# Windows of the large convolutions loaded during the last image's own layers, and paired products for dt and the normaliser

## The chip, the cores and the metric

The kernel runs on 1 core of a Trainium2 chip. The metric is the device time of one execution in microseconds. Three runs of the kernel before took 5239.56 us in the median (5237.0 to 5242.91). All data are f32. The engines are PE (matrix products), PEld (its weight loads), DVE (vector), ACT (scalar), POOL (GpSimd) and SP, which only issues transfers. DMAs are issued by SP, by ACT and by POOL.

## The reference

`x` is (8, 384, 32, 32): eight images, 384 channels, 1024 pixels. Four layers follow each other.

```python
# layer 0: RMS norm, a selective scan over the 1024 pixels in both directions, a 3x3 depthwise gate
def mamba(x, ...):
    u, z = split(x @ in_proj.T);  u = silu(causal_conv1d(u, 4 taps) + b)
    dt, Bm, Cm = split(u @ x_proj.T, [24, 40])            # 24, 16, 16
    delta = softplus(dt @ dt_proj.T + dt_b)
    h = exp(delta * A) * h + (delta * u) * Bm              # 16 states, pixel after pixel
    return ((h * Cm).sum(states) + u * D) * silu(z) @ out_proj.T
x_norm = rmsnorm(x)
g = (mamba(x_norm) + flip(mamba(flip(x_norm)))) * scale_mod
x = x + res_scale * (g + sigmoid(dwconv3x3(x_norm)) * x_norm)
# layer 1: bn, 1x1, 3x3 depthwise, bn, 1x1, residual; linear attention of 8 heads; layer norm and MLP
x1 = conv1x1(bn(dwconv3x3(conv1x1(bn(x))))) + x
q, k, v = split(conv1x1(x1));  qp, kp = phi(q), phi(k)     # phi(t) = exp(.5 * (2t - t*t))
z = 1 / (qp . kp.sum(pixels) + eps)                        # the normaliser
x2 = x1 + conv1x1((qp @ (kp.T @ v)) * z)
x = x2 + gelu(ln(x2) @ w1 + b1) @ w2 + b2                  # 384 -> 1536 -> 384
# layer 2: seven depthwise convolutions (13x13, 5x5, 7x7, dilated ones), each with its bn, summed
x = sum(bn_j(dwconv_j(x)))
# layer 3: 1x1 with bn and residual, then 13x13 depthwise and a scale per channel, each with bn
xp = bn(conv1x1(x)) + x
out = gelu(bn(dwconv13x13(xp)) + bn(xp * dw1_w))
```

## The kernel before

Everything is in two functions. `tile_layers` makes the constants, calls `_layers01` for layers 0 and 1, and then computes layers 2 and 3 for all eight images at once.

**Layers 0 and 1, image by image.** `front(b)` makes what the scan of image b needs: the norm, `in_proj`, the local 3x3 gate, the short convolution, `x_proj` and, per half image and 128 channels, two products `dt` (one per direction, with 24 rows of weights each that lie at partitions 0 and 64), softplus, and delta (`dlt`) and delta times u (`vr`), which go to DRAM. `scan(b)` walks over units of a direction, a half image and 128 channels; each has four rounds of four states. A round loads `dlt`, `vr` and `bct` (B and C) in a form repeated over the states, and computes `da` (ACT, L782), `du` (DVE, L787), the scan `hs` (DVE, L799), `hs` times C (POOL, L808) and the sum over states `acc` (PE). `layer1(b)` then does the rest of layer 0 and layer 1: `op` (out_proj, added to `xx` by DVE at L891), `h` into the padded image `hh` (its edge columns are set by POOL in `image6`, L526; it is put into DRAM `h_d` by ACT, L532), the 3x3 depthwise `dw` from `dw_i` (SP loads, L543), `c2`, keys and values, queries, the normaliser `den` (six products at L1005, for the two half images in two column groups of PE), its reciprocal `rz` and the product `rzb` (L1017) that spreads it over the channels, `pj`, the layer norm, and the MLP (`mf`, `hm`, `mo`), whose result goes to DRAM `x2_d` (POOL, L1070).

**What sets the order.** Each engine's order is made by the scheduler of the Tile framework from the order in which the program is written and from the buffers of the pools. A planner in `_layers01` writes it: it steps through the scans of images 0 to 7, and between rounds it advances generators (`front(b+1)`, `layer1(b-1)`, `fold`, `prepare`) whose costs and due times are in `jobs`. `defer` and `tick` put small DVE work some steps later. `together(products, made)` keeps a list of products side by side on PE: the first is held behind the instructions `made`, and the others follow with a high priority (`AHEAD`) in program order. Before the change it is used for the 32-column products (`col32`), for `x_proj` and for `acc`. Image 7's `layer1` has no other image beside it:

```python
        tick(everything=True)
        for _ in seconds[B - 1]:
            tick()
        tick(everything=True)
```

**Layers 2 and 3.** During image 1's scan `kernels` (driven as `prepare`) merges layer 2's seven kernels into one 13x13 kernel per channel, in DRAM as `g2_d`, and layer 3's 13x13 and its scale as `g3_d`. A convolution `conv(g_d, src_d, tag, put)` runs over 96 groups of 4 channels. `xt` holds rows of the images (32 rows on 32 partitions, loaded by POOL at L281, then copied by DVE at L289 to three more blocks of 32 partitions, each shifted by a column). `tp` holds the Toeplitz windows, which the load makes out of the kernel by overlapping reads from DRAM in runs of 512 bytes, two blocks by SP and two by ACT. Both tiles cover 16 channels and have three buffers. A group is 16 products (4 taps, 4 channels, 32 columns each; they count twice in the profile) into one of six PSUM tiles `cv`. Convolution a reads `x2_d` and stores `yt` to `y2_d` (POOL, L319). The pointwise stage follows in 16 steps: a load `yp` (SP), nine products `pw` (L333), `tm` (ACT), the residual into `xo` (DVE; the three `xo` tiles are set to zero by POOL at L243 ahead of convolution a), and a store to `xp_d` (POOL, L347). Convolution b reads `xp_d`, and each group ends with a gelu into `ot` (ACT, L353, three buffers) and a store to `out` in runs of 128 bytes (POOL, L354). `pbias`, a small bias product, stands ahead of convolution a.

The tiles of these stages come out of pools that are opened after those of `_layers01` are closed, so they lie in the same memory and have to wait for its last users.

Of the kernel before, what the change touches and what calls it, by code (L numbers as in the profile page):

```python
# [10 lines left out]
FP = mybir.dt.float32  # L11
# [28 lines left out]
N_A6, N_T2, N_S2, N_W, N_IM = 7, 9, 3, 4, 8  # L40
N_REP, N_DA, N_HS = 6, 4, 8
# [26 lines left out]
def tile_layers(  # L68
# [95 lines left out]
    def kernels(small, large):  # L164
# [60 lines left out]
        with nc.allow_non_contiguous_dma(reason="384 biases"):  # L225
# [3 lines left out]

    _layers01(tc, nc, B, xv, x2_d, dram, ident, mean_w, eps5, eps6, one, half, minus1, vec, bns, bnt,  # L230
              rs, rsm, inproj_t, xproj_t, dtproj_t, outproj_t, taps1, taps3, taps3b, sel, alog,
              cw1_t, cw2_t, qkv_t, proj_t, w1, w2, headmask, mask8, mask8_t, kernels)
# [4 lines left out]
    with tc.tile_pool(name="cw", bufs=1) as cwp, tc.tile_pool(name="cx", bufs=2) as cxp, tc.tile_pool(  # L237
        name="cps", bufs=6, space=PSUM
# [11 lines left out]

        pbias = cwp.tile([P, NC, 1], FP, tag="pbias", name="pbias")
        for m in range(NC):
            ps = cps.tile([P, HALF], FP, tag="cv", name=f"pb_{m}")
            for k in range(NC):
                nc.tensor.matmul(
                    ps[:, 0:1], pwt[:, k, m * P : (m + 1) * P], bias2[:, k, :],
                    start=(k == 0), stop=(k == NC - 1),
                )
            nc.vector.scalar_tensor_tensor(
                pbias[:, m, :], ps[:, 0:1], bns("pw", m), bnt("pw", m), ALU.mult, ALU.add  # L260
            )
            nc.vector.tensor_add(pbias[:, m, :], pbias[:, m, :], bias2[:, m, :])

        def conv(g_d, src_d, tag, put):
# [3 lines left out]
            NCH = 4 * GB  # L268
            xt = tp = None
            for g in range(NQ):  # L270
                if g % GB == 0:
                    xt = cxp.tile([P, NCH, RL], FP, tag="xt", name=f"xt_{tag}_{g}", bufs=3)
                    tp = cxp.tile([P, NCH, TP], FP, tag="tp", name=f"tp_{tag}_{g}", bufs=3)

                    q0 = g // GB % 2 * 2
                    at = [H * ((q0 + e) % NSH) for e in range(NSH)]
                    src = bass.AP(
                        src_d.tensor, src_d[4 * g, 0, 0].offset,
                        [[RL, H], [H * RL, NCH], [1, RL]],
                    )  # L280
                    nc.gpsimd.dma_start(xt[at[0] : at[0] + H], src)  # L281
                    for e in range(NSH):
                        win = bass.AP(
                            g_d.tensor, g_d[4 * g, e, 0, 0].offset,
                            [[KT, H], [NSH * TG * KT, NCH], [1, TP]],
                        )
                        (nc.scalar if e % 2 else nc.sync).dma_start(tp[at[e] : at[e] + H], win)
                    for n in (1, 2):
                        nc.vector.tensor_copy(  # L289
                            xt[at[n] : at[n] + n * H, :, 0 : RL - n - (n - 1)],  # L290
                            xt[at[0] : at[0] + n * H, :, n : RL - (n - 1)],
                        )
                ps = cps.tile([P, HALF], FP, tag="cv", name=f"cv_{tag}_{g}")
                for t in range(KT):
                    for e in range(4):
                        c = 4 * (g % GB) + e
# [25 lines left out]

        yf = y2_d.rearrange("(k p) h b w -> p k (h b w)", p=P)
        xf = xp_d.rearrange("(k p) h r -> p k h r", p=P)
        NB = 2 * BW
        for t in range(H // 2):
# [20 lines left out]
            nc.gpsimd.dma_start(xf[:, :, 2 * t : 2 * t + 2, :], xo)  # L347

# [12 lines left out]
def _layers01(tc, nc, B, xv, x2_d, dram, ident, mean_w, eps5, eps6, one, half, minus1, vec, bns, bnt,  # L361
              rs, rsm, inproj_t, xproj_t, dtproj_t, outproj_t, taps1, taps3, taps3b, sel, alog,
              cw1_t, cw2_t, qkv_t, proj_t, w1, w2, headmask, mask8, mask8_t, kernels):
# [10 lines left out]
    with ExitStack() as ctx:  # L374
        wp = ctx.enter_context(tc.tile_pool(name="w0", bufs=1))
        sp = ctx.enter_context(tc.tile_pool(name="s0", bufs=2))
        accp = ctx.enter_context(tc.tile_pool(name="acc0", bufs=1, space=PSUM))
# [196 lines left out]
        def front(b):  # L574
# [56 lines left out]
            for h in range(2):  # L631
# [37 lines left out]
                for c in range(NC):  # L669
                    dls = []  # L670
                    for d in range(2):
                        ps = psum(f"dt_{b}_{h}_{d}_{c}")
                        at = slice(64 * d, 64 * d + DTR)
                        nc.tensor.matmul(
                            ps, wdt[at, c * P : (c + 1) * P], xd[at, :], start=True, stop=True
                        )
                        dl = t2(f"dl_{b}_{h}_{d}_{c}")
                        nc.scalar.activation(dl, ps, AF.Softplus, bias=vec("dt_b", c))
                        dls.append(dl)
# [15 lines left out]
        def scan(b):  # L695
# [10 lines left out]
            def load_bc(k, r):  # L706
                d, h, _ = units[k]
                t = sp.tile([P, 2, HALF], FP, tag="bct", name=f"bct_{b}_{d}_{h}_{r}", bufs=4)
# [8 lines left out]
            def load(k, i):  # L717
# [3 lines left out]
                for src_d, n in ((dl_d, "dlt"), (v_d, "vr")):  # L721
                    t = sp.tile([P, 2 * HALF], FP, tag="rep", name=f"{n}_{b}_{d}_{h}_{c}_{i}", bufs=N_REP)
# [38 lines left out]
            for k, (d, h, c) in enumerate(units):  # L761
                cols = bass.ts(h, HALF)
                second = k % (2 * NC) >= NC
                for r in range(NR):
# [12 lines left out]
                    for i in range(2):  # L777
                        dlt, vt = now[i]
                        da = sp.tile([P, 2 * HALF], FP, tag="da", name=f"da_{b}_{k}_{r}_{i}", bufs=N_DA)
# [15 lines left out]
                        t = sp.tile([P, 2 * HALF], FP, tag="hs", name=f"hs_{b}_{k}_{r}_{i}", bufs=N_HS)  # L795
# [80 lines left out]
        def layer1(b):  # L876
# [126 lines left out]
            for k in range(NC):  # L1003
                for h, at in enumerate(ats):
                    nc.tensor.matmul(  # L1005
                        den[at, :], ksv[:, k, :], qps[h][:, k, :], start=(k == 0), stop=(k == NC - 1),
                        skip_group_check=True,
                    )
            for at in ats:
                nc.scalar.activation(rz[at, :], den[at, :], AF.Ln, bias=eps6[at])  # L1010
            for at in ats:
                nc.scalar.activation(rz[at, :], rz[at, :], AF.Exp, scale=-1.0)
            yield 3
            for k in range(NC):
                for h, at in enumerate(ats):
# [192 lines left out]
```

## Time and profile before

| | |
|---|---|
| runs shown | 5239.56 us median of 3 |
| the profiled execution | 5247.45 us, span 5245.7 us |
| instructions | 57987 |
| busy PE, PEld | 4292.2 us (82%), 1772.1 us (34%) |
| busy DVE, ACT, POOL | 3793.6 us (72%), 2739.8 us (52%), 2911.7 us (56%) |
| mean granted clock of PE | 0.9 |
| DMA | 975.07 MB, mean 186 GB/s |

The stages after the last scan, in us from the span's start, by the instructions of the tiles named:

| stage | from | to |
|---|---|---|
| image 7's own layers | 4207 | 4574 |
| convolution a, products `cv_a` | 4594.75 | 4814.15 |
| pointwise, products `pw` | 4827.84 | 4953 |
| convolution b, products `cv_b` | 4971.5 | 5241 |

How to read it: the page lists the busy time of each engine over the whole span, and that of 40 equal slices; a group of instructions is a source line, an engine, an operation and its tiles, with a count and the mean of one. A busy share over the whole span mixes stages that have different limits, so each stage is read by itself. A wait is given to the one that released it last. A DMA share over 1 means that the packets of a stretch took longer, summed, than 16 engines have time: packets in flight lie over one another.

### The profile page before, as it was taken

What the parts mean: (1) busy time and instruction counts of PE and PEld (TensorE: products, weight loads), DVE (VectorE), ACT (ScalarE), POOL (GpSimd) and SP (SyncE); (2) the same over time, 40 slices, a digit from 0 to 9 for tenths busy, and PEclk for the clock granted to TensorE, in tenths of its full rate; (3) what the DMA queues carried; (4) which work ended last, traced back from release to release, by engine and by line L of the source; (5) the groups of instructions that cost most, each with busy time, mean ns of one, the idle gap of its engine ahead of it and who ended that gap; (6) DMA issues with size and microseconds to landing.
All of it is one profiled execution on the core that took longest, in us unless ns stands there. A gap on an engine that the chain in (4) does not pass through costs nothing. (4 is left out here: it accounts for less than half of the span.)

```text
span 5245.7 us, 57987 instructions
## 1 busy us (share of the span) xinstructions
PE 4292.2 (82%) x20128; PEld 1772.1 (34%) x20128; DVE 3793.6 (72%) x3765; ACT 2739.8 (52%) x3816; POOL 2911.7 (56%) x1472
## 2 busy tenths in 40 slices
PE   4675568888988998898889888998788879787877
PEld 1121123233333333333333333333233324365455
DVE  0399899987888788878887889788879901065344
ACT  1455544785578557755775677468536603001211
POOL 3276666676667665766675667566767800111155
PEclk7686679899989998999899999999889999899988
DMA  9866447666757674767567646765644541499698
GB/s 280 253 198 209 167 146 217 205 202 177 213 190 208 177 222 168 224 179 218 176 199 203 213 168 196 211 204 183 160 150 137 147 105 38 79 235 219 193 197 168
DMA packets 560045, 975.07 MB, mean 186 GB/s; under 512 B 53208, under 2 KB 238024, under 8 KB 559752
## 3 DMA queue, kind: packets, MB, share of 16 engines
q1 hardware_dynamic: 410992, 669.13, 42.8%
q0 software_dynamic: 56800, 205.10, 15.2%
q10 hardware_dynamic: 91960, 97.14, 6.8%
q8 instruction: 159, 2.61, 0.2%
q14 instruction: 134, 1.10, 0.1%
HBM read 726.36 MB, written 244.81 MB: 185 GB/s over the span
## 5 line engine op out<-in xcount | busy, mean ns | idle before, releaser
L808 POOL TENSOR_TENSOR hs<-hs,bct 128x1024 f32<-128x1024 f32 x768 | 2410.7, 3139 | 1001.1 <-DVE carry L804 470.6
L782 ACT ACTIVATE da<-dlt,neg_a 128x512 f32<-128x512 f32 x1536 | 1035.6, 715 | 775.7 <-DVE hs L799 718.5
L799 DVE TENSOR_TENSOR_SCAN hs<-da,du 128x512 f32<-128x512 f32 x768 | 902.4, 1209 | 248.7 <-ACT da L782 146.3
L787 DVE TENSOR_TENSOR du<-vr,bct 128x1024 f32<-128x1024 f32 x768 | 1059.3, 1379 | 29.0 <-DMA vr<-v_d 18.5
L799 DVE TENSOR_TENSOR_SCAN hs<-da,carry,du 128x512 f32<-128x512 f32 x768 | 944.1, 1267 | 56.4 <-PE acc L506 14.4
L506 PE MATMUL acc<-hs,selt 128*32 128x512 f32 x2304 | 560.5, 658 | 189.8 <-POOL hs L808 189.7
L1058 PE MATMUL mo<-hm,w 128*128 128x512 f32 x1152 | 572.0, 637 | 91.1 <-ACT hm L1056 89.4
L489 PE MATMUL mf<-ln,w 128*128 128x512 f32 x1152 | 565.6, 627 | 11.7 <-DMA w<-w_d 11.7
L501 PE MATMUL acc<-hs,selt 128*32 128x512 f32 x768 | 419.5, 645 | 72.8 <-POOL hs L808 46.8
L1058 PEld LDWEIGHTS mo<-hm,w 128*128 128x128 f32 x1152 | 219.4, 200 | 438.3 <-issue 240.3
L782 ACT ACT_TABLE_LOAD x278 | 356.7, 1283 | 7.6 <-ACT hh L899 2.7
L489 PEld LDWEIGHTS mf<-ln,w 128*128 128x128 f32 x1152 | 222.4, 200 | 334.3 <-issue 314.3
L489 PE MATMUL in<-xn,win 128*128 128x512 f32 x576 | 293.0, 640 | 12.0 <-ACT uz L603 7.7
L301 PE MATMUL cv_b<-xt_b,tp_b 128*32 128x256 f32 x3072 | 203.9, 424 | 83.3 <-ACT ot L353 60.6
L1070 POOL DMA_DIRECT2D x_d<-xx x48 | 56.4, 1177 | 350.6 <-DVE xx L1067 350.5
L289 DVE COPY xt_b<-xt_b 32x4992 f32<-32x4992 f32 (+1 forms) x48 | 135.0, 2813 | 131.8 <-DMA xt_b<-xp_d 131.0
L1056 ACT ACTIVATE hm<-mf,biasf 128x512 f32<-128x512 f32 x192 | 131.9, 687 | 179.6 <-PE mf L489 177.8
L301 PE MATMUL cv_a<-xt_a,tp_a 128*32 128x256 f32 x3072 | 182.3, 389 | 47.0 <-issue 37.1
L506 PE MATMUL dw<-dw_i,t3b 96*32 96x512 f32 x1056 | 207.5, 637 | 4.1 <-DMA dw_i<-h_d 3.6
L301 PEld LDWEIGHTS cv_b<-xt_b,tp_b 128*32 128x32 f32 x3072 | 150.8, 143 | 136.8 <-ACT ot L353 71.2
L506 PEld LDWEIGHTS acc<-hs,selt 128*32 128x32 f32 x2304 | 92.7, 114 | 301.3 <-POOL hs L808 281.0
L354 POOL DMA_DIRECT2D out<-ot x96 | 130.4, 1363 | 113.4 <-ACT ot L353 113.1
(194 smaller groups left out, 5771.4 us busy)
## 6 DMA issues: line engine op xcount, KB each, us to landing
dlt<-dl_d SPq DMA_DIRECT2D x384, 256.0 KB, 4.2
vr<-v_d SPq DMA_DIRECT2D x384, 256.0 KB, 4.9
bct<-bc_d SPq DMA_DIRECT2D x256, 256.0 KB, 3.8
ut<-u_d SPq DMA_DIRECT2D x192, 257.5 KB, 5.6
lc_i<-xn_d SPq DMA_DIRECT2D x192, 228.8 KB, 5.5
dw_i<-h_d SPq DMA_DIRECT2D x192, 228.8 KB, 4.5
w<-w_d SPq DMA_DIRECT2D x64, 576.0 KB, 6.1
w<-in_w SPq DMA_DIRECT2D x64, 576.0 KB, 5.4
```

The costliest lines, as they stand in the source:

```text
L289: nc.vector.tensor_copy(xt[at[n] : at[n] + n * H, :, 0 : RL - n - (n - 1)], xt[at[0] : at[0] + n * H, :, n : RL - (n - 1)],)
L301: nc.tensor.matmul(ps[H * e : H * (e + 1), 0:BW], tp[:, c, :].rearrange("p (j t) -> p j t", t=KT)[:, :, t], rhs, start=(t == 0), stop=(t = ...
L354: nc.gpsimd.dma_start(ov[g * P : (g + 1) * P], ot.rearrange("p (b w) -> p b w", w=W))
L489: nc.tensor.matmul(ps, w[:, k, m * P : (m + 1) * P], rhs[k] if isinstance(rhs, list) else rhs[:, k, :], start=(k == 0), stop=(k == NC - 1),)
L501: first = product()
L506: tc.keep_in_program_order(product())
L782: nc.scalar.activation(da[:, bass.ts(j, HALF)], dlt[:, bass.ts(j, HALF)], AF.Exp, scale=neg_a[:, g, r : r + 1],)
L787: nc.vector.tensor_mul(pairs(du), pairs(vt), bct[r][:, 0:1, :].to_broadcast([P, 2, HALF]),)
L799: nc.vector.tensor_tensor_scan(t[:, s][:, way], da[:, s][:, way], du[:, s][:, way], k_c if second else 0.0, ALU.mult, ALU.add,)
L808: made.append(nc.gpsimd.tensor_mul(pairs(t), pairs(t), bct[r][:, 1:2, :].to_broadcast([P, 2, HALF])))
L1056: nc.scalar.activation(hm, ps, AF.Gelu, bias=biasf[:, NC * i + f, :])
L1058: nc.tensor.matmul(acc[m], wb[:, f, m * P : (m + 1) * P], hm, start=(i == 0 and f == 0), stop=(i == FF // C - 1 and f == NC - 1),)
```

## The change

It does four things.

1. The scan's tiles `bct`, `rep`, `da` and `hs` move from the pool `s0` to a pool `scan` of their own, on the right side of the memory. That pool is closed before image 7's `layer1`. A pool `win` is opened in its place, with 20 tiles of 8 channels (`N_WIN`, `NCH`).
2. A generator `windows` loads the first 20 windows of convolution a through POOL's queue, advanced once per step of image 7's `layer1`.
3. `conv` takes windows of 8 channels, and `xt` of 8 channels with four buffers (before: 16 channels and three buffers for each). It asks for windows up to ten blocks ahead through SP and ACT. The pointwise loop asks for one window of convolution b per step. `pbias` is moved behind convolution a. The pools `cw`, `cx` and `cps` are opened with `reuse_waits="tile"`: each of their tiles waits for the users of its own place and not for those of the whole pool.
4. The two `dt` products, the six of `den` and the two `rzb` of each k go through `together`.

The core of the diff (the body of `put2`, of the products' loop and of `conv`'s addresses is moved unchanged, and left out):

```diff
+N_WIN, NCH = 20, 8
+    NB_C = C // NCH
+    wins = {}
+    def load_windows(g_d, tag, n, queues):
+        if not wins:
+            wins["pool"] = ctx.enter_context(tc.tile_pool(name="win", bufs=1, side="right"))
+        tp = wins["pool"].tile([P, NCH, TP], FP, tag="tp", name=f"tp_{tag}_{n}", bufs=N_WIN)
+        for e in range(NSH):
+            at = H * ((n % 2 * 2 + e) % NSH)
+            win = bass.AP(
+                g_d.tensor, g_d[NCH * n, e, 0, 0].offset,
+                [[KT, H], [NSH * TG * KT, NCH], [1, TP]],
+            )
+            queues[e % len(queues)].dma_start(tp[at : at + H], win)
+        wins[tag, n] = tp
+
+    def windows(queues):
+        for n in range(N_WIN):
+            load_windows(g2_d, "a", n, queues)
+            yield
...
-    with tc.tile_pool(name="cw", bufs=1) as cwp, tc.tile_pool(name="cx", bufs=2) as cxp, tc.tile_pool(
-        name="cps", bufs=6, space=PSUM
+    with tc.tile_pool(name="cw", bufs=1, reuse_waits="tile") as cwp, tc.tile_pool(
+        name="cx", bufs=2, reuse_waits="tile"
+    ) as cxp, tc.tile_pool(
+        name="cps", bufs=6, space=PSUM, reuse_waits="tile"
     ) as cps:
...
         def conv(g_d, src_d, tag, put):
-            NCH = 4 * GB
             xt = tp = None
             for g in range(NQ):
-                if g % GB == 0:
-                    xt = cxp.tile([P, NCH, RL], FP, tag="xt", name=f"xt_{tag}_{g}", bufs=3)
-                    tp = cxp.tile([P, NCH, TP], FP, tag="tp", name=f"tp_{tag}_{g}", bufs=3)
+                n, first = divmod(4 * g, NCH)
+                if first == 0:
+                    xt = cxp.tile([P, NCH, RL], FP, tag="xt", name=f"xt_{tag}_{n}", bufs=4)
                     ...
                     nc.gpsimd.dma_start(xt[at[0] : at[0] + H], src)
-                    for e in range(NSH):
-                        win = bass.AP(...)
-                        (nc.scalar if e % 2 else nc.sync).dma_start(tp[at[e] : at[e] + H], win)
+                    for m in range(n, min(n + 1 + N_WIN // 2, NB_C)):
+                        if (tag, m) not in wins:
+                            load_windows(g_d, tag, m, [nc.sync, nc.scalar])
+                    tp = wins[tag, n]
...
             nc.gpsimd.dma_start(xf[:, :, 2 * t : 2 * t + 2, :], xo)
+            if t < N_WIN:
+                load_windows(g3_d, "b", t, [nc.scalar, nc.sync])
...
+        scan_ctx = ExitStack()
+        scanp = scan_ctx.enter_context(tc.tile_pool(name="scan", bufs=1, side="right"))
...
-                    for d in range(2):
-                        ps = psum(f"dt_{b}_{h}_{d}_{c}")
-                        at = slice(64 * d, 64 * d + DTR)
-                        nc.tensor.matmul(
-                            ps, wdt[at, c * P : (c + 1) * P], xd[at, :], start=True, stop=True
-                        )
+                    pss = [psum(f"dt_{b}_{h}_{d}_{c}") for d in range(2)]
+                    together([
+                        partial(
+                            nc.tensor.matmul, pss[d], wdt[64 * d : 64 * d + DTR, c * P : (c + 1) * P],
+                            xd[64 * d : 64 * d + DTR, :], start=True, stop=True,
+                        )
+                        for d in range(2)
+                    ], [])
+                    for d, ps in enumerate(pss):
                         dl = t2(f"dl_{b}_{h}_{d}_{c}")
...
-            for k in range(NC):
-                for h, at in enumerate(ats):
-                    nc.tensor.matmul(den[at, :], ...)
+            together([
+                partial(nc.tensor.matmul, den[at, :], ksv[:, k, :], qps[h][:, k, :], ...)
+                for k in range(NC) for h, at in enumerate(ats)
+            ], [])
...
-                nc.scalar.activation(rz[at, :], rz[at, :], AF.Exp, scale=-1.0)
+                made = nc.scalar.activation(rz[at, :], rz[at, :], AF.Exp, scale=-1.0)
             yield 3
             for k in range(NC):
-                for h, at in enumerate(ats):
-                    ps = long_psum(f"rzb_{b}_{h}_{k}")
-                    nc.tensor.matmul(ps, wdt[at, bass.ts(k, P)], rz[at, :], start=True, stop=True)
+                pss = [long_psum(f"rzb_{b}_{h}_{k}") for h in range(2)]
+                together([
+                    partial(nc.tensor.matmul, ps, wdt[at, bass.ts(k, P)], rz[at, :], start=True, stop=True)
+                    for ps, at in zip(pss, ats)
+                ], [made])
+                for h, ps in enumerate(pss):
                     nc.vector.tensor_mul(qps[h][:, k, :], qps[h][:, k, :], ps)
...
+        scan_ctx.close()
+        ahead = windows([nc.gpsimd])
         for _ in seconds[B - 1]:
             tick()
+            next(ahead, None)
+        for _ in ahead:
+            pass
         tick(everything=True)
```

## The prediction

> **What bounds the kernel now.** I read the page's 40 slices first, then the table of busy time by stage, then the waits and groups of the last 700 us. Up to 4.2 ms the eight images' scans run beside the layers of their neighbours; there no engine is alone the limit. In the rows below the columns are the stretch, its length, busy time of PE, PEld, DVE, ACT and POOL, the granted clock, the DMA share and GB/s.
>
> ```profile
> 2000.00:3000.00 1000.00, 879.41 (x3340) 329.18 (x3338) 836.50 (x820) 660.63 (x896) 651.18 (x293) 0.94 0.65 195
> 4225.00:4575.00 350.00, 295.66 (x879) 127.94 (x877) 29.62 (x43) 66.32 (x107) 7.43 (x7) 0.92 0.31 67
> 4595.00:4814.00 219.00, 181.90 (x3072) 156.97 (x3064) 142.88 (x94) 17.50 (x47) 40.85 (x44) 0.98 1.11 235
> 4828.00:4955.00 127.00, 125.28 (x288) 55.11 (x288) 36.59 (x96) 37.33 (x48) 11.26 (x15) 0.99 0.64 205
> 4971.00:5241.00 270.00, 203.94 (x3072) 150.79 (x3072) 129.97 (x47) 45.37 (x96) 147.05 (x116) 0.88 0.93 179
> ```
>
> Read the DMA share down: 0.31 in the last image's own layers, 1.11 in the first large convolution, 0.64 in the pointwise stage (PE-bound, 125 of 127 us), 0.93 in the second convolution. Who fills the first convolution is told by the queues of 4600 to 4800 us (packets, MB, share of 16 engines):
>
> ```profile
> q0 software_dynamic: 6048, 24.47, 43.5%
> q1 hardware_dynamic: 23162, 11.50, 34.2%
> q10 hardware_dynamic: 23121, 11.48, 33.2%
> ```
>
> q0 is POOL's (rows of x and stores), q1 and q10 are SP's and ACT's: only Toeplitz windows. So windows take 67 of 111. PE runs 128 products in 7.46 us and then idles 1.4 to 2.2 us; 24 x 7.46 = 179 us is its floor for a stage of 219.4 us (4594.75 to 4814.15).
>
> In the second convolution the end is set by something else, as the waits from 4950 on show (engine and line, what it waited for: us, times, longest):
>
> ```profile
> ACT ot L353 <- DMA out<-ot: 175.0, 67, 9.7
> PE cv_b L301 <- ACT ot L353: 60.6, 21, 5.3
> ```
>
> ACT waits for one of three ot buffers, that is for a store to land; PE waits for ACT. The tile's own view says how long a landing takes (min, median, max):
>
> ```profile
> DMA to landing us min/median/max: 2.9/7.5/10.1
> ```
>
> A ring of three gives 3 groups per 0.47 (ACT) + 0.89 (issue) + 7.5 + some 0.3 = 9.2 us, 3.05 a group. The starts of ACT's evictions agree: 79 groups from 4982.90 to 5222.51 are 3.03 us each. The last window load is issued at 5210.0; from 5222.51 on, 12 groups take 18.1 us, 1.51 each. **Windows on the other two queues slow the stores' landing; without them PE's 1.87 us a group is the floor.**
>
> **What the skill says.** "DMA: Bandwidth & Descriptors", section "Queues, rings and completion order": each DMA engine goes round-robin between queues, a packet at a time. The trace agrees in kind: packets of 4.0 KB on q0 and 0.5 KB on q1 and q10 share the 16 engines. Same page, "SWDGE vs HWDGE vs iDMA": GpSimd writes the descriptors of its DMAs in state that VectorE's fast mode locks it out of. Out issues take 885 ns at least and 3456 at most, and an xt_b issue at 5055.32 took 3.21 us. "TensorE: Matmul & The Clock Gate", "The mechanism" of Part 3: products in different row or column groups run together. den does so in the trace: 12 instructions in 2.77 us, where 12 in a row would take 12 x 0.43 = 5.2.
>
> **The change, part by part.** The order of the changed program on each engine, which I read as built, decides more than the diff.
>
> *Windows ahead, last image (+10 us).* 80 loads of 128 KB go onto POOL, after the last x_d stores (4223.8) and around the hh memsets: 28 before the first, 12 more before the second. Nearest issues: xt 0.67 us with 512 runs; a window has 256, so I take 0.67: 28 are 19 us, 40 are 27. ACT puts the images at 4262.4 and 4270.1, so memsets at 4243 and 4251 would be hidden. But each POOL DMA waits for the one eight before it, so issues go at transfer speed: 22.98 MB took 0.674 x 200 us, 170 GB/s; 10.5 MB take 62 us, from 4238 (when the queued x_d stores have landed) to 4300. The memsets then come at about 4238 + 20 x 0.77 = 4253 and 4238 + 32 x 0.77 = 4263, still covered. Not covered is the sharing: g (8.2 us, PE waits 15.75), two h_d puts (5.8 us to the first dw_i) and 24 dw_i loads (23.6 us) run in those 62 us. If sharing doubled them all it would be +30; if it costs nothing 0. I take +2, +3, +5.
>
> *Start of the first convolution (-13 us).* Now: all queues free at 4574.3, xo memsets to 4579.3, xt lands 4586.8, two copies 5.5 us, PE at 4594.75 waiting for windows: 20.45 us. After: the memsets wait only for PE and hardware queues, not for x2's stores, so they lie beside those stores' landing (14.5 us); windows are there; xt has 8 channels. 0.67 + 4 (half of 7.5) + 2 x 1.37 + 0.2 = 7.6. Bounds -8 to -15.
>
> *First convolution (-10 us).* The order shows what the ring of 20 does: window 20+i is loaded by SP and ACT when block i ends, and after the 28 left of g2 come 20 of g3. So a window is still loaded in every one of the 48 blocks: 0.524 + 0.321 (x) + 0.262 (y) = 1.107 MB a block, 242 GB/s at 4.57 us. What goes is the gating of a three-deep ring: the new xt ring of four gives 3.73 + 0.3 + 0.67 + 8 + 2.75 = 15.5 us per four blocks, 3.9 each, so bytes decide. At the best slice of the stage's 20-us table, 254 GB/s: 4.36 x 48 = 209. Bounds: 0 (same rate) and -40 (PE's floor). Doubled issues: 24 more xt on POOL, 16 us in a stage with 178 idle; 48 more on each of SP and ACT at 0.36 us, idle too.
>
> *Gap, pointwise stage (0 us).* pbias (18 products, 4 us of PE) moves into the 13.7 us in which PE waits for yp; SP has the first 20 windows of g3 ahead of yp in its order, the last of them free only as the stage ends; before, three 16-channel tiles stood there. No window is loaded in the pointwise stage. Bounds -5 to +8.
>
> *Start of the second convolution (-4).* From 4955.2 to 4971.5: landing 5.6 to 4, copies 5.5 to 2.75.
>
> *Second convolution (-28).* 20 of its 48 windows are there; 28 are loaded in blocks 0 to 27, so groups up to about 58 are slow and 38 free: 5 x 2 + 53 x 3.03 + 38 x 1.87 = 242 against 270. Bounds: -15 (free groups at 2.4) and -50 (loaded groups at 2.6, since xt bursts ahead of the stores are halved).
>
> *dt and den pairs (-8).* Most pairs stand side by side already; the built order changes two of six dt pairs an image and the last den product, 3 x 0.86 us of PE per image, some 15 us of an engine that is 88% busy. More comes from the reordering that follows: at each hand-over of images DVE now sits at L891 waiting 11.5 us for op (1.62 + 4.40 + 3 x 1.82); after, two scan pairs stand ahead of it, but op's last one no longer hides. I take -8; bounds -35 and +20, as the scheduler moves some 600 DVE rows and I can't price them.
>
> Sum: +10 - 13 - 10 - 4 - 28 - 8 = **-53**. The profiled execution took 5247.45 us (span 5245.7 and 1.75 around it), 7.9 above the median of 5239.56; I set the gain against the median: 5186.6, say **5187**.
>
> **Rivals.** *(1) PE floor in both convolutions (0.13):* a 20-deep ring lets windows lag while xt gets its share; -40 and -50 instead of -10 and -28, so -105, 5135. For: PE's chain needs only 3.9 us a block. Against: a share of 1.11 in every slice of the stage. *(2) Only moved (0.12):* every block still loads a window, out landing stays 7.5 us to the end of the queue's backlog; only the starts and 12 us remain: +10 - 17 - 12 - 3 = -22, 5218. *(3) Slower, by POOL's queue (0.06):* the hh memsets sit behind 28 and 40 window loads. The rest of the change gains 63; the second memset has 47 us before 4270.1, so at (47 + 63)/40 = 2.75 us per load the gain is gone. Out issues of up to 3.46 us exist; at 3.46 the memset is at 4362, 92 late: +29, 5269. Against: DVE is 8% busy there, nothing to lock POOL out. *(4) No effect (0.04):* reordering of the scans costs what the end gains; 5240. The forecast, with its own sizes moving, has 0.65.
>
> **Numbers.** A measurement of this kernel can't tell less than about 0.2% (10 us) from no change. The sum's own bounds, taken as independent, give about 30 us each way; (1) and (2) widen that to 5140 to 5226, leaving out (3), (4) and half of (1). Faster: 0.65 + 0.13 + 0.11 = 0.89; same 0.05 (4 and a little of 2); slower 0.06.
>
> **What would show it.** Right: first cv_a product less than 10 us after x2's last store lands; DMA share in the first convolution still above 1; ACT's waits for out down from 175 us, and the last 38 groups under 2.2 us each; dw products 10 us later after the last scan. Wrong: cv_a stage under 195 us (rival 1), last groups at 3 us (rival 2), hh memsets after 4270 (rival 3), hand-overs of images not 508.7 us apart but several us more or less (the scan term).

## The result, and the profile after

The changed kernel takes 5253.82 us in the median (5246.56 to 5270.52, 7 runs) against 5242.13 us (5237.0 to 5244.89, 7 runs) of the kernel before on the same chip: a ratio of 1.0032 with a 95% interval of 1.0020 to 1.0044, 12 us slower. 5187 was forecast.

Its profiled execution took 5267.59 us, 13.8 above its median, with a span of 5265.8; the profile before lay 5.3 above the median of its seven runs. So the two spans differ by 20.1 us where the medians differ by 11.7. Cut at the same landmarks (the last `hs` scan, the last `dw` product, the last `mo` product, the first and last `cv_a`, the first `cv_b`, the end of the span), the 20.1 us lie here:

| stretch, us | before | after | change | term of the prediction |
|---|---|---|---|---|
| start to the last scan | 4194.5 | 4228.3 | +33.8 | -8 |
| last scan to last `dw` | 114.0 | 139.2 | +25.2 | +10 |
| last `dw` to last `mo` | 247.8 | 248.9 | +1.1 | 0 |
| last `mo` to first `cv_a` | 38.5 | 28.1 | -10.4 | -13 |
| convolution a | 219.0 | 216.5 | -2.5 | -10 |
| last `cv_a` to first `cv_b` | 157.7 | 149.7 | -8.0 | -4 |
| first `cv_b` to the end | 274.2 | 255.1 | -19.1 | -28 |

The end of the kernel did get faster, by 38.9 us from the last `dw` on. Two stretches ahead of it took 59.0 back. These are the rows of busy time by stage that answer to those of before; the columns are the same.

```profile
2000.00:3000.00 1000.00, 867.82 (x3193) 327.41 (x3188) 814.75 (x812) 624.71 (x856) 629.66 (x285) 0.92 0.64 191
4260.00:4610.00 350.00, 299.17 (x863) 127.12 (x862) 27.31 (x40) 65.68 (x106) 47.93 (x83) 0.89 0.45 95
4644.50:4861.50 217.00, 186.71 (x3074) 160.13 (x3074) 155.93 (x142) 17.55 (x48) 72.20 (x67) 0.97 1.07 236
4871.00:4997.00 126.00, 125.75 (x288) 55.43 (x288) 35.83 (x94) 36.55 (x47) 11.45 (x15) 0.98 0.66 207
5010.00:5261.00 251.00, 195.39 (x3072) 161.11 (x3072) 141.55 (x95) 45.47 (x96) 153.02 (x139) 0.93 0.79 166
```

In the first row every engine does less in the same 1000 us: PE 868 against 879, DVE 815 against 837. The scans go slower, and no engine is fuller for it. The third row still shows a DMA share over 1, in the last it fell from 0.93 to 0.79.

The granted clock of the first row fell too, from 0.94 to 0.92. Between 1200 and 3750 us some kinds of product take as long as before (`kv_kp` 497 and 496 ns, `lc` 595 and 595, `in` 622 and 625), while `mo`, which waits for `hm`, takes 671 ns in place of 635. Whether the lower clock follows from longer waits of PE or adds to the loss, no run separates.

Where the scans lose time is read from DVE's waits between the first and the last hand-over of images (1200 to 3750 us). The columns are who waited for what: us, times, longest. First the kernel before:

```profile
DVE hs L799 <- ACT da L782: 126.9, 42, 13.7
DVE hs L799 <- PE acc L506: 64.4, 24, 5.6
DVE xx L891 <- PE op L489: 57.4, 25, 4.4
...
DVE xn L588 <- PE ms_b L566: 5.0, 4, 2.4
```

Then the changed kernel:

```profile
DVE hs L827 <- ACT da L810: 111.4, 31, 11.9
DVE hs L827 <- PE acc L531: 78.2, 32, 8.0
DVE xx L919 <- PE op L514: 55.7, 25, 4.4
DVE xn L613 <- PE ms_b L591: 31.9, 7, 8.8
...
DVE hs L827 <- PE acc L526: 11.3, 3, 4.8
DVE xn L613 <- DMA dlt<-dl_d: 8.2, 1, 8.2
```

The wait for `op`, on which the prediction had its eye, is the same. `xn` for `ms_b` grew most: 35 us more with the 8.2 that the view puts down to `dlt`. `acc` grew from 69.2 (with a line of 4.8 for L501) to 89.5. Scan by scan, the changed kernel falls back by 8 to 12 us in the first 24 scans after each of the hand-overs to images 2 to 6, and wins 10 back at the last one, beside which no front runs. The same place shows in DVE's idle time, taken from the last scan of an image to the 25th of the next and summed over these five hand-overs: 109 us before, 138 after. This sum is used again below.

`ms_b` belongs to the norm of the next front, which starts with the load `xi`. Two answers for the tile `xi` at the same hand-over (before, after), and two for the stores of `x2` there (before, after):

```profile
L580 SPq DMA_DIRECT2D xi<-in_x x2: 373/376/379, 2135.0 to 2165.7; - x2
DMA to landing us min/median/max: 4.8/5.4/6.1
```

```profile
L605 SPq DMA_DIRECT2D xi<-in_x x2: 368/371/374, 2177.5 to 2199.3; - x2
DMA to landing us min/median/max: 6.1/14.0/21.9
```

```profile
L1070 POOL DMA_DIRECT2D x_d<-xx x3: 1159/1193/1223, 2144.0 to 2148.7; - x3
```

```profile
L1102 POOL DMA_DIRECT2D x_d<-xx x3: 1154/1182/1203, 2172.7 to 2178.5; - x3
```

Before, `xi` went out at 2135.0, 9 us ahead of the first x2 store (2144.0). After, it goes out at 2177.5, 5 us behind it, and lands 21.9 us later; those stores take 12.5 to 20.7 us to land. That was my first theory of the loss; the experiments did not leave it standing.

### The profile page after: what moved, and what is told of

It is laid out like the page before. It is cut to its first block, busy times and chain, and to the rows that moved or that the text cites. A ratio compares the mean times of both kernels' runs of the same rounds, so it can differ in the third digit from the quotient of the medians.

```text
span 5265.8 us, 58411 instructions
## 1 busy us (share of the span) xinstructions
PE 4313.9 (82%) x20128; PEld 1795.6 (34%) x20128; DVE 3815.2 (72%) x3861; ACT 2683.7 (51%) x3772; POOL 2991.7 (57%) x1600
## 5 line engine op out<-in xcount | busy, mean ns | idle before, releaser
L815 DVE TENSOR_TENSOR du<-vr,bct 128x1024 f32<-128x1024 f32 x768 | 1067.1, 1389 | 28.1 <-DMA vr<-v_d 17.8
L1090 PE MATMUL mo<-hm,w 128*128 128x512 f32 x1152 | 594.8, 661 | 122.6 <-ACT hm L1088 112.7
L296 DVE COPY xt_b<-xt_b 32x2496 f32<-32x2496 f32 x96 | 143.9, 1499 | 114.1 <-DMA xt_b<-xp_d 107.9
L308 PEld LDWEIGHTS cv_a<-xt_a,tp_a 128*32 128x32 f32 x3072 | 160.0, 139 | 84.8 <-issue 32.4
```

What stands on the lines that cost most here:

```text
L296: nc.vector.tensor_copy(xt[at[e] : at[e] + e * H, :, 0 : RL - e - (e - 1)], xt[at[0] : at[0] + e * H, :, e : RL - (e - 1)],)
L308: nc.tensor.matmul(ps[H * e : H * (e + 1), 0:BW], tp[:, c, :].rearrange("p (j t) -> p j t", t=KT)[:, :, t], rhs, start=(t == 0), stop=(t = ...
L815: nc.vector.tensor_mul(pairs(du), pairs(vt), bct[r][:, 0:1, :].to_broadcast([P, 2, HALF]),)
L1090: nc.tensor.matmul(acc[m], wb[:, f, m * P : (m + 1) * P], hm, start=(i == 0 and f == 0), stop=(i == FF // C - 1 and f == NC - 1),)
```

## The experiments

Each is set against runs of the kernel before on its own chip; from chip to chip the kernel before took 5242 to 5282 us in the median, so only ratios and differences within a chip are compared. The label of a run stands ahead of its edit.

### Which part moves the scans

**e1_dt_pair_only**, on the kernel before:

```diff
-                    for d in range(2):
-                        ps = psum(f"dt_{b}_{h}_{d}_{c}")
-                        ...
+                    pss = [psum(f"dt_{b}_{h}_{d}_{c}") for d in range(2)]
+                    together([partial(nc.tensor.matmul, pss[d], ...) for d in range(2)], [])
```

> The kernel before with one edit: the two dt products of a pair go through together. Theory A (the dt pair moves the built order of the scans; the load xi of the next front then goes out after the first x2 store of the hand-over instead of 9 us ahead of it, and lands with it, and DVE stands 8 to 12 us for ms_b in each of images 2 to 6): the last scan ends 30 to 36 us later than in the kernel before, time +15 to +35 us. Rival B (the scan's tiles in a pool of their own on the other side of the memory cost it): within 5 us of the kernel before.

Measured: ratio 1.0064 (1.0049 to 1.0079), +32.6 us. The last scan ends 40.9 us later than in the kernel before; 9.5 us of that stand ahead of the first scan of all, where e3, which leaves dt alone, has them too. The idle time at the five hand-overs is 135 us. In the trace at least 193 of DVE's 3525 instructions ahead of the large convolutions stand in another place, counted by the tiles' names; in e3 and e9 none does. Yet in each of images 2 to 7 only two of six dt pairs did not stand side by side before, and the edit brings one of them together.

**e2_no_dt_pair**, the changed kernel with that edit undone:

> The changed kernel with the dt products as they were before. Theory A: the last scan ends within 4 us of the kernel before, xi lands in under 7 us again; what is left is the end: +26 in image 7's own layers, -10 at the start of convolution a, -2 in it, -8 in the pointwise stage, -19 in convolution b, so 13 us faster than before, 5225 to 5233. Rival B: the last scan is still 30 us late, and the time is that of the changed kernel, some 5254.

Measured: 0.9965 (0.9951 to 0.9979), -14.7 us. The six loads `xi` between 1620 and 2760 us land in 4.5 to 6.2 us again.

**e3_scan_pool_only**, on the kernel before:

```diff
+        scanp = scan_ctx.enter_context(tc.tile_pool(name="scan", bufs=1, side="right"))
-                t = sp.tile(..., tag="bct", ...)        # and rep, da, hs
+                t = scanp.tile(..., tag="bct", ...)
```

> The kernel before with one edit: bct, rep, da and hs in a pool of their own on the right side, closed ahead of image 7's layer1; nothing is put in its place. Theory A: within 5 us of the kernel before. Rival B: last scan 30 us later, time +15 to +35 us.

Measured: 0.9998 (0.9989 to 1.0006). The pool costs nothing; rival B is out.

**e9_den_rzb_only**, on the kernel before: only den and rzb go through `together`.

> The kernel before with one edit: den's six products and the rzb pairs go through together, dt as before. As built it moves one den product per image on PE and nothing on any other engine. Theory (standing side by side costs nothing, only a moved order of the scans does): within 6 us of the kernel before, at best 7 us faster (one product of 0.86 us an image). Rival (held pairs make PE wait): 10 us or more slower.

Measured: 0.9982 (0.9975 to 0.9990), -10 us by the medians. Standing side by side is a small gain where it moves nothing else.

So the whole loss in the scans is the dt pair's. The next run asks whether it is the pair, or the order around it.

**e10_dt_pair_without_priority**, on the kernel before:

```diff
+                    for d in range(2):
+                        tc.keep_in_program_order(nc.tensor.matmul(pss[d], ...))
```

> The kernel before with the two dt products of a pair written one after the other and kept in program order, without the high priority that together gives the second. As built 42 of 48 pairs stand side by side, as many as in the dt pair alone, but the order of the scans is a third one: at the hand-over of images acc stands ahead of the last op again, as in the kernel before, and xi is about as late on SP as with the dt pair. Theory C (the order of acc and op at the hand-over costs, not the pair): the wait of hs for acc there is back to 3 us from 12, and the time is 0 to 15 us over the kernel before. Rival D (the pair costs by itself, by taking both PSUM buffers at once): 30 us or more over it.

Measured: 1.0099 (1.0086 to 1.0112), +53 us. Theory C had both the wait and the time wrong. It forecast that the wait of `hs` for `acc` at the hand-over goes back to 3 us. Ahead of the first scan of each of images 2 to 6 DVE stands 14.6 to 16.6 us for `acc`, where it is 5.6 in the kernel before and 1.6 to 5.8 in e1. PE and DVE at the hand-over to image 4 show it (start and length in us; in brackets the idle time before, and what ended it):

```profile
2260.81 5.31 PE L1059 MATMUL mo<-hm,w 128*128 128x512 f32 x12
2265.96 2.74 PE L489 MATMUL in<-xn,win 128*128 128x512 f32 x6
2268.63 0.63 PE L506 MATMUL acc<-hs,selt 128*32 128x512 f32 x3
```

```profile
2269.89 2.33 DVE L800 TENSOR_TENSOR_SCAN hs<-da,du 128x512 f32<-128x512 f32 x2 [16.57 <-PE acc L506]
```

POOL has finished what `acc` sums at 2255.5. `acc` then stands on PE for 13 us behind `mo` and `in`, and the next scans stand behind `acc`. The first scans alone cost 49 us more than in the kernel before, and the idle time at the five hand-overs is 161 us. A second place shows in the waits of ACT and of DVE over 1200 to 3750 us:

```profile
ACT da L783 <- DMA dlt<-dl_d: 73.5, 9, 13.9
```

```profile
DVE hs L800 <- PE acc L506: 108.8, 20, 16.6
...
DVE zr L756 <- PE acc L506: 49.0, 13, 9.9
```

In this order the scan's own loads `dlt` stand on SP behind the second `xi`, which waits for x2's stores to land, and ACT stands for them (1.9 us in all in the kernel before); `zr` waits 49.0 us for `acc` where it was 8.6. Some of this is won back at the last hand-over.

Rival D forecast 30 us or more, and the time lies there. This edit, like e1, makes both PSUM tiles of a pair at once, and it brings as many pairs together (42 of 48 in both, 36 before). It loses more than e1, and most of the loss has a place: `acc` behind `mo` and `in`. So the order in which products stand on PE is shown to cost 49 us here; that a pair has no price of its own beside it is not shown.

### Whether one wait carries the dt pair's cost

The stores of x2 have runs of 128 bytes. Written in runs of 2 KB they land fast, and `xi` can't be held by them. They go to a tile that nothing reads, so convolution a computes on zeros and doesn't wait for them.

```diff
-                        nc.gpsimd.dma_start(x2v[m, :, h * (H // 2) : ..., PADW + ... ], rows(o))
+                        nc.gpsimd.dma_start(chunks(x3_d)[b][:, m, bass.ts(h, HALF)], o)
```

**e6_dt_pair_short_stores** and **e7_no_dt_pair_short_stores**:

> The changed kernel, dt pair included, with x2's stores written in runs of 2 KB to a DRAM tile that nothing reads, in place of runs of 128 bytes to x2 (convolution a then reads the zeros that were put there). SP's order, and so the place of xi in it, is that of the changed kernel. Theory (what the dt pair costs is xi landing together with slow x2 stores): xi lands in under 8 us, ms_b waits of 8 to 12 us at the hand-overs are gone, and the last scan ends within 5 us of the next kernel's. Rival (the order of the dt pair costs by itself, through PSUM or ACT): the last scan ends 30 us after the next kernel's.

> The same edit of the stores on the changed kernel without the dt pair. Theory: same end of the scans as with the dt pair, within 5 us; both a little under 4194 since the hh memsets no longer wait for landings of 17 us. Rival: 30 us ahead of the kernel with the dt pair.

Measured: 0.9935 (0.9910 to 0.9960) with the pair, 0.9869 (0.9846 to 0.9891) without it. With the pair `xi` lands in 4.3 to 8.1 us (six loads, 1620 to 2760 us), DVE's wait for `ms_b` and `dlt` between 1200 and 3750 us falls from 40 to 17 us, and the dt pair still costs 34 us by the medians, with some 18 us either way. My theory fell.

The same two kernels made from the kernel before, **e13_before_short_stores** and **e14_dt_pair_short_stores**, and both again with two of three `op` products left out, so that `acc` has less to stand behind, **e15_short_stores_op_cut** and **e16_dt_pair_short_stores_op_cut**:

```diff
-                    dense(ps, w, m, gh)
+                    nc.tensor.matmul(ps, w[:, 0, m * P : (m + 1) * P], gh[:, 0, :], start=True, stop=True)
```

> The kernel before with x2's stores written in runs of 2 KB to a DRAM tile that nothing reads (convolution a then reads zeros). The reference for the next run. Theory E and rival F alike: 20 to 40 us under the kernel before, since convolution a need not wait for those stores, and the SP wait of xi for them goes from 54 us in all to under 15.

> The same with the dt pair. Theory E (the pair costs two waits of like size, xi behind the stores and acc behind op): 10 to 22 us over e13, not 33; ms_b waits under 18 us in all between 1200 and 3750 us, acc waits 20 to 26 us over those of e13. Rival F (only the order at the hand-over costs; the wait for xi hides other idle time and its going brings nothing): 28 us or more over e13.

> e13 with two of three op products left out (only the first 128 of 384 inputs of out_proj are used): PE has 20.5 us less to do per image at the hand-over. Reference for the next run: 60 to 140 us under e13, where the wait xx<-op of 11.5 us an image goes.

> e15 with the dt pair. Theory E (what is left after the stores is acc behind op): acc waits within 10 us of those of e15 between the first and last hand-over, and 0 to 10 us over e15. Rival G (other places of the moved order cost as well): 15 us or more over e15 with acc waits alike, and the place shows in the groups that DVE waits for.

Measured: 0.9852 (0.9834 to 0.9870) and 0.9911 (0.9894 to 0.9928), so the pair costs 31 us, as rival F had it. The stores themselves were mispriced: 20 to 40 us were expected for e13, and it is 75 us under the kernel before. Its trace is 38 us shorter than that of the kernel before, which is from another chip; where the rest lies is not known. With `op` cut it is 0.9733 (0.9715 to 0.9751) and 0.9820 (0.9801 to 0.9840), so the pair costs 42 us. The waits of DVE in e15 and in e16, over 1200 to 3750 us:

```profile
DVE hs L800 <- ACT da L783: 127.5, 36, 15.3
DVE hs L800 <- PE acc L507: 53.9, 19, 5.9
```

```profile
DVE hs L803 <- ACT da L786: 104.0, 32, 9.8
DVE hs L803 <- PE acc L507: 85.8, 34, 8.3
...
DVE xx L921 <- PE c L490: 21.9, 10, 3.9
...
DVE xn L589 <- PE ms_b L567: 15.9, 6, 3.6
```

A third of `op` is all that is left, and `acc` waits are still some 22 us up (e15 has another 9.7 at L502). `c`, with 12.3 us in e15, is up by 10, and `ms_b` by 12. Theory E is out as it was put on record. `acc` can stand behind other products, as it stands behind `mo` and `in` in e10, and this cut doesn't touch them. Of rival G the time is as told; the `acc` waits are not alike, but other waits grow beside them, and the cost stays where one of them is taken away.

What is shown is that the dt edit costs 31 to 42 us in four settings, that DVE's idle time at the five hand-overs grows by 22 to 26 us in each of them, and that neither slow landings nor the length of `op` carries it. That the moved order does it is the reading that fits these runs; which step of that order starts it stays open.

### The windows ahead

**e4_windows_after_dw**, on the changed kernel:

```diff
     def load_windows(g_d, tag, n, queues, gate=None):
+        if gate is not None:
+            nc.gpsimd.tensor_copy(tp[:, 0, 0:1], gate)     # gate: a column of image 7's last dw
```

> The changed kernel, with the 20 windows ahead held back until image 7's last dw eviction: a one-column copy of dw into each window's tile on POOL comes before its load (20 small instructions). Theory (the 10.5 MB share the DMA engines with g, the h_d puts and dw_i): the 26 us between the last scan and the last dw product come down to under 4, and the loads now run beside the key and value stage; time 18 to 26 us under the changed kernel, some 5232. Rival (the loads cost the same wherever they are put, since weights are loaded throughout the image): the stage from dw to mo grows by what the stage ahead loses, time within 6 us of the changed kernel.

Measured: 0.9974 (0.9963 to 0.9984) of the kernel before, where the changed kernel had 1.0032 on its chip: 30 us by the two ratios. In its trace, last scan to last `dw` takes 114.8 us (114.0 before the change, 139.2 after), and last `dw` to last `mo` 247.7, as ever. Begun 29 us after the last scan, as in the changed kernel, the loads cost 25 us; begun at 118 us, as here, nothing. What they collided with is told by the DMA issues of the 88 us from the first window load on in the changed kernel (KB each, median us to landing), and of the same stretch before:

```profile
tp_a<-g_d POOLq DMA_DIRECT2D x80, 128.0 KB, 7.3
dw_i<-h_d SPq DMA_DIRECT2D x12, 228.8 KB, 11.8
```

```profile
dw_i<-h_d SPq DMA_DIRECT2D x24, 228.8 KB, 4.6
```

Twelve of the 24 `dw_i` loads fall into this stretch after the change, and land in 11.8 us where it was 4.6.

**e5_no_dt_pair_windows_after_dw**, both cures in one:

> Both changes of the earlier runs in one kernel: the dt products as before, and the 20 windows ahead held back until image 7's last dw eviction. Theory (the two costs are separate and add): -15 from the run without the dt pair and -24 from the windows, 36 to 42 us under the kernel before, ratio 0.992 to 0.993; stages op to first dw 60 us and dw 28 us. Rival (each alone already removed a shared cost): about 20 us under the kernel before, ratio 0.996.

Measured: 0.9898 (0.9882 to 0.9915), -54 us (45 to 62), more than the 36 to 42 expected. From the last scan to the end it takes 1012.0 us against 1051.2 in the profile before, the 39 expected. The rest lies in the scans, where e9 has 10 us for the den and rzb pairs that this kernel keeps; that it adds up so is argued across chips, not shown.

### The two convolutions

**e8_b_windows_in_pointwise**, on e5:

```diff
-                load_windows(g3_d, "b", t, [nc.scalar, nc.sync])
+                load_windows(g3_d, "b", t, [nc.gpsimd], yt[:, 0, 0:1])
```

> The kernel without the dt pair and with windows after dw, in which the first 16 windows of convolution b are loaded by POOL in the pointwise stage, each behind a one-column copy of that step's yp, and not during convolution a. Theory (convolution a is bound by bytes, 1.107 MB a block at some 240 GB/s): it moves 32 windows in place of 48, 45 MB in place of 53, and comes down by 25 to 33 us, to 187 to 194 us; the pointwise stage takes 8.4 MB more in 127 us, and grows by 0 to 20 us. Rival (convolution a is bound by the order of its xt loads and copies): it stays at 215 to 220 us.

Measured: 0.9912 (0.9897 to 0.9927); convolution a takes 215.9 us, e5's 216.7. Two rows of it, 20 us each:

```profile
4640.00:4660.00 20.00, 17.28 (x297) 15.35 (x301) 13.35 (x13) 1.49 (x4) 7.59 (x8) 1.00 1.14 240
4720.00:4740.00 20.00, 17.74 (x309) 15.62 (x304) 15.73 (x15) 1.86 (x5) 5.83 (x7) 1.00 0.42 119
```

The second has no window loads left. The DMA share falls from 1.14 to 0.42, and PE does 309 products in place of 297. The rows between differ as much, so the last quarter of the stage tells more: without a window load a group takes 2.15 us in it, and with them 2.20 (e5). Bytes do not bound this stage. The time as a whole is no better than e5's. **e17_xt_ring_of_six**, on e12 below (`bufs=4` to `bufs=6` for `xt`), asks about the ring:

> e12 with six xt buffers in place of four in both convolutions. Theory (POOL's loads of xt wait for PE to free one of four, and DVE's copies and PE then stand in one chain): convolution a comes down from 217 us by 10 to 30 us. Rival (DVE's two copies a block and its evictions, some 3.3 us of 4.5, or PE itself set the pace): under 5 us.

Measured: convolution a takes 220.1 us (e12: 217.4), the time is 0.9816 (0.9799 to 0.9832) where e12 has 0.9825. A deeper ring alone doesn't help. It wasn't put to full use, though. POOL issues the loads of `xt` in order with the stores of `yt`, and with six buffers a load goes out 9.5 us after its buffer comes free (median; 1.0 with four). What sets the pace is open. Per block of 4.5 us PE works 3.7 and DVE 3.3 (two copies of 1.45, an eviction of 0.42), and a block's first product starts 0.2 us after its second copy ends (median), so the copies are in the chain. Stores of `yt` by another engine were not tried.

**e11_conv_b_without_reloads**, on e5:

```diff
+        if tag == "b" and n >= N_WIN:
+            wins[tag, n] = wins[tag, n - N_WIN]
+            return
```

> The kernel without the dt pair and with windows after dw; convolution b uses its first 20 windows again for the other 28 blocks, so 28 loads of 0.52 MB are left out. Theory (loads slow the landing of the out stores, and with it the groups up to 58): those groups come down from 2.76 us to the 2.3 us of the free ones, convolution b by 22 to 30 us. Rival (POOL's issues and DVE's copies set the pace with or without loads): by under 10 us.

Measured: 0.9881 (0.9867 to 0.9895). From the first `cv_b` to the end 238.0 us against e5's 256.5, -18.5: between the two. The groups up to 58 take 2.50 us (e5: 2.65), the rest 2.28 (2.54). e5's 2.54 is high for a kernel with loads: the changed kernel has 2.26 there, e8 2.29. So what the later groups gained here may be chance, and this run doesn't decide between loads and POOL.

**e12_out_stores_by_sp**, on e5:

```diff
-            nc.gpsimd.dma_start(
+            nc.sync.dma_start(
                 ov[g * P : (g + 1) * P], ot.rearrange("p (b w) -> p b w", w=W)
```

> The kernel without the dt pair and with windows after dw; the stores of out are issued by SP in place of POOL. Theory (POOL, with 0.89 us per out store and up to 2 us where DVE copies, holds the free groups at 2.3 us): free groups at 1.9 to 2.0 us, convolution b 20 to 35 us shorter. Rival (the landing of a store in a ring of three ot buffers holds them): within 5 us of the same kernel with POOL's stores, or slower where a store stands behind a window load on SP.

Measured: 0.9825 (0.9813 to 0.9838), -91 us; first `cv_b` to the end takes 210.4 us, 46 less than e5 and more than the 20 to 35 expected. Groups take 2.34 us up to 58, and 1.82 after it. The tile `ot` in the changed kernel, and in e12:

```profile
L377 POOL DMA_DIRECT2D out<-ot x96: 885/892/2176, 5015.1 to 5261.4; - x96
...
DMA to landing us min/median/max: 2.9/4.7/8.9
```

```profile
L379 SPq DMA_DIRECT2D out<-ot x96: 372/404/3725, 4951.3 to 5154.1; - x96
...
DMA to landing us min/median/max: 2.3/5.2/9.9
```

The landing is no faster (5.2 against 4.7 us). The issue is, but POOL's time isn't the whole of it: POOL stands idle for much of the stage, waiting for the next `ot`, and the loads of `xt` stand behind that wait in its order. The waits of e5 from 4940 us on, and of e12 from 4950 on:

```profile
POOL out L379 <- ACT ot L378: 102.6, 69, 8.9
DVE xt_b L298 <- DMA xt_b<-xp_d: 95.0, 38, 7.5
```

```profile
POOL xt_b L292 <- PE cv_b L310: 133.4, 36, 10.9
DVE xt_b L298 <- DMA xt_b<-xp_d: 57.0, 33, 4.9
```

In e5 a load of `xt` goes out 7.2 us after its buffer comes free (median), and a block's first product starts 0.1 us after its second copy ends: landing, copies and products stand in one chain. In e12 the load goes out after 0.3 us, and the copies end 3.6 us ahead of the product. How the 46 us divide between this and the shorter issue wasn't tried. What is left in e12 is the ring of `ot`:

```profile
ACT ot L378 <- DMA out<-ot: 138.3, 82, 4.9
```

**e18_ot_ring_of_six**, on e12 (`bufs=3` to `bufs=6` for `ot`):

> e12 with six ot buffers in place of three. Theory (with POOL out of the way, the landing of 5.2 us in a ring of three holds a group at 0.47 + 0.4 + 5.2 + 0.3 over 3 = 2.1 us): groups at PE's 1.9 us, convolution b from 210 to 185 to 200 us, 10 to 25 us under e12. Rival (the DMA share of 1.1 sets the pace while windows are loaded): under 6 us.

Measured: 0.9798 (0.9770 to 0.9826), first `cv_b` to the end 203.6 us, 7 less than e12 and between the two forecasts. Its interval and e12's meet, so the step itself is not clear of noise; the kernel is, at 5139.33 us against 5247.66, the fastest of all, ahead of both that the case began with.

## Why the prediction was wrong

**dt and den pairs: -8 taken, +33.8 in the trace and +32.6 us for the dt pair alone.** This step decides the sign. The prediction had seen in the built order that two scan pairs move ahead of `op` at the hand-over, and that 600 DVE rows move. It then gave that a gain, from a wait for `op` of 11.5 us an image that did not change (57.4 and 55.7 us in all), and bounds of -35 and +20 for what it could not price. What came in its place is a loss at five hand-overs: the waits for `acc` grew by 20 us and those for `ms_b` by 35, the image-to-image time rose from 507.8 to 516.5 us on average (images 2 to 7), as the prediction's own sign of being wrong had it, and the cause within the moved order stays open. The den and rzb pairs, in the same term, gained 10 us (e9). The bound was too narrow, and rival 4, in which the reordering of the scans costs what the end gains, had 0.04. It came nearest: 5240, with the end's gain of 39 us spent on the scans and the windows.

**Windows ahead: +10 taken, +25.2 measured**, inside its bounds. The mechanism was right, sharing with `g`, the `h_d` puts and `dw_i`; each of the three terms was too small. The wait for `g` grew by 3.6 us (2 taken). The `h_d` puts landed in 8.4 to 13.0 us (3.7 to 5.8 before), and the first `dw` came 10.7 us later after the last `hh` (3 taken). The `dw` products took 38.7 us for 29.3 (5 taken). The loads also went on for 83 us, from 4257.6 to 4340.3, where 62 were taken: the last x2 stores of image 6 were still landing, and only seven loads could go out in the first 18 us.

**Rival 3, POOL's queue, did not happen.** The `hh` memsets came at 4291.5 and 4302.4, each ahead of its half's evictions (4295.4 to 4308.3). The result is on that rival's side for another reason.

**Start of convolution a: -13 taken, -10.4 measured.** xt goes out when x2's stores have landed, as told, and the first product follows 9.5 us later, not 7.6.

**Convolution a: -10 taken, -2.5 measured.** "So bytes decide" is the step that failed. The rate stayed at 236 GB/s where 254 was taken, but e8 shows that the rate was not the limit. A DMA share over 1 was read as a full resource; it meant that packets were in flight, and the windows among them held nothing up.

**Pointwise and the gap: -4 taken together, -8.0 measured**, within the bounds.

**Convolution b: -28 taken, -19.1 measured.** The groups up to 58 take 2.81 us, better than the 3.03 taken; the later ones take 2.26, not PE's 1.87. "Without them PE's 1.87 us a group is the floor" left out POOL, which issues the stores in 0.89 us or more each and, after the change, twice as many xt loads, in one order. e12 shows it. The last twelve groups of the kernel before, at 1.51 us, were no sign of a free rate: PE made its last nine in 19.1 us, 2.1 each, and ACT emptied PSUM tiles that were full already; nor had they an xt load beside them (POOL issued the last at 5207.1).

## What to carry to other kernels

An edit to a few products of a scheduled kernel is priced by what it does to the order of everything else: count what moves first, and give its bound both signs and the size of the waits at the seams, some 10 us for each of five hand-overs here. A load that is moved ahead isn't free by itself: put behind the last `dw` it cost nothing here, put ahead of it 25 us. A busy DMA share names no limit: ask who waits for a transfer, who issues it, and what stands ahead of it in the issuer's order.

## What the runs showed of the hardware

A store of 128 KB to `out` takes 885 ns or more of POOL's time to issue and 372 of SP's. A store that waits for its data holds the loads that the same engine issues after it: with the stores on POOL a load of `xt` went out 7.2 us after its buffer was free, with the stores on SP 0.3 us. Moving the 96 stores took 46 us out of a stage of 256 (e5 and e12). Nothing in the landing times (4.7 and 5.2 us) hinted at it.

Two kernels with the same work on every engine, in which only products stand in another order as written (e9 and e10), differ by 1.2% on one chip (0.9982 and 1.0099).
